# Two attention layers on one core: the steps of layer 1's convolution taps, and of the weight mixes, are set anew

## The chip, the cores and the metric

One core of a Trainium2 chip. The time is that of the whole program on the device, in microseconds. Its engines are TensorE (PE, with its weight loads as PEld), VectorE (DVE), ScalarE (ACT), GpSimd (POOL) and SyncE (SP). Each runs its own queue of instructions in order, and semaphores tie them together. In this kernel SP and POOL issue the DMAs.

## The reference

Two residual layers on an image batch of 4 x 32 x 32 tokens with 768 channels. Each is `x + attention(group_norm(x))` with 12 heads of 64. Layer 0 is plain; layer 1 passes q, k and v through a 3x3 depthwise convolution and a layer norm over each head's 64 channels before it attends. Both add a bias of relative position, by rows and by columns.

```python
# layer 0
q = heads(x @ Wq + bq); k = heads(x @ Wk + bk); v = heads(x @ Wv + bv)
attn = einsum('bqd,bkd->bqk', q, k) / sqrt(HD) + rel_bias_h + rel_bias_w
out = softmax(attn) @ v ; return out @ Wp + bp
# layer 1
q = layer_norm(dwconv3x3(q, w_pool_q), g_q, b_q)    # k and v alike
attn = einsum('bqc,bkc->bqk', q * scale, k) + rel_h + rel_w
o = softmax(attn) @ v + q ; return o @ w_proj.T + b_proj
```

## The kernel before

**Stages and pairs.** There are eight stages, in this order: layer 0 of images 0 and 1, layer 1 of images 0 and 1, then the same for images 2 and 3. A stage has six pairs of heads. Pairs are numbered 0 to 47 over all stages; a pair's index in its stage (`hp`) is that number modulo 6. So layer 1 is pairs 12 to 23 and 36 to 47.

**Steps.** The order on PE, DVE, ACT and POOL is written out by hand. `attend` is a generator that gives a pair's attention in four quarters. A quarter is four score tiles (L1091 with the bias added in L1093), four exponentials (L1098, ACT), and then the product with v (L1115). After the scores it yields twice, and after the product twice, so a pair has 16 steps, and pair i's attention covers the steps 16i to 16i+15. The first quarter of a pair has its steps 0 to 3, and so on. At each step the pieces that `at` has put there are emitted. A piece is work that belongs to a later pair, to the projection of the stage before, to the group norm of the stage after, or to the weights. Pieces of one step are emitted in the order in which they were registered: group norm and token sums first, then the weight mixes, then the pairs' pieces, then the projection's.

**What is prepared when.** `Pair.plan` gives for pair i a list of pieces with steps counted from 16(i-1). So a step of 0 or more lies in the attention of the pair before, and a step of -8 to -1 in the second half of the one before that. In layer 1 that is: q and k by matrix products at -8 to 0, q's nine taps, k's taps, `centre(Q)` at 3 (PE transposes, DVE L721 and L722), `square` and `squares` of q (L728 on ACT, L732 and L733 on DVE), `norm(Q)` at 7 or 8 (the logarithm and exponential L160 and L162 on ACT, then L164 to L167 and L744 on DVE), `back(Q)` at 9 (PE L753, ACT L558 and L559), and the same for k from 8 to 14. `split` (step 12) writes the bias of position in two parts, `high` (L791) and `whole` (L792), which POOL sends to the bias tiles by DMA (L802). v's taps, centring, squares and norm run at 8 to 15.

**The seven products.** Where pair i and the two before it are all of layer 1 (`in_products`; 20 pairs: indexes 2 to 5 of the stage of the first layer-1 image, 0 to 5 of the second, in each half), q and k come from seven products of half-size weights and token sums (`products`, steps -8 or -7 to 0). These need sums of weights ("late" mixes, u = 15 + hp) and sums of tokens in DRAM, read as `blocks` by `call`, L605. With q's padded image complete at -5 (or at -6 for indexes 1 and 4), q's nine taps start: L704 or L702 is the first tap (DVE or ACT), L706 each of the others, over 128 x 1056 elements. A second pair of buffers for the padded image and the convolved one is taken in turn.

**Mixes.** `mix_weights(u)` loads two weight blocks (SP, 384 KB each, into the ring `wproj` of two buffers), and at a later step makes four or five sums or differences of them on DVE (L316 or L328), each of which SP stores to DRAM. u = 0 to 8 are for layer 0's products, 9 to 11 for its projection, 12 to 14 for layer 1's projection, 15 to 20 for layer 1's products. All run once, in the first half of the program: the list at L1295 has for each u the step of the loads and the step of the sums.

**Projection.** In the first 20 steps of a stage the projection of the stage before runs in parts (`four`, `three`; PE L138 with p1p to p7 as output, L1203 and L1198 on DVE, which empty the banks). At the steps 11, 15 and 19 of a stage that leads to or is layer 1, the loop at L1325 puts the pieces marked `taps` of that step between the two parts of the projection.

**Banks.** Score tile 1 of a quarter takes the PSUM area `place_b`, tile 2 `place_c`; between the scores other products use these areas in halves. A score tile therefore waits until the last reader of the halves is done. Tiles 0 and 3 share an area, so tile 3 waits for the first exponential.

**SP's queue** isn't ordered by hand: its order is set by a scheduler when the program is built.

## Time and profile before

| | us |
|---|---|
| time, median of 3 runs (lowest to highest) | 3794.95 (3792.31 to 3801.69) |
| profiled execution, its own time | 3800.9 |
| its span | 3798.9 |

Length of the stages, from the first score matmul of one to that of the next, and how much of it TensorE was idle in gaps over 0.15 us (worked out from the trace's instructions):

| stage (layer, image) | pairs | us | PE idle, us |
|---|---|---|---|
| 1 (0, 1) | 6 to 11 | 464.6 | 5.7 |
| 2 (1, 0) | 12 to 17 | 492.4 | 13.2 |
| 3 (1, 1) | 18 to 23 | 487.3 | 18.4 |
| 5 (0, 3) | 30 to 35 | 460.4 | 3.0 |
| 6 (1, 2) | 36 to 41 | 495.0 | 13.3 |
| 7 (1, 3) | 42 to 47 | 511.8 | 19.7 |

Length of the quarters of some pairs, in us, and the pair's sum:

| pair | index prepared at steps 0 to 15 | quarters | sum |
|---|---|---|---|
| 13 | 2 | 33.8, 13.3, 26.3, 16.1 | 89.5 |
| 14 | 3 | 14.9, 13.3, 26.8, 15.6 | 70.6 |
| 15 | 4 | 18.3, 13.7, 28.7, 15.7 | 76.5 |
| 16 | 5 | 15.6, 13.3, 30.3, 15.6 | 74.8 |
| 17 | 0 | 14.7, 13.3, 26.2, 15.6 | 69.9 |
| 18 | 1 | 19.2, 13.3, 47.5, 38.8 | 118.9 |
| 39 | 4 | 19.8, 13.8, 30.1, 17.3 | 81.0 |
| 45 | 4 | 18.9, 13.3, 27.0, 15.6 | 74.9 |

How to read the profile's lines: in a timeline, the start in us from the span's start, the duration, the engine, the line of the kernel, the operation, what it writes and reads, how many instructions were merged, and in brackets the idle time of the engine before it and what ended it. In a table of windows: the window, its length, then the busy time and (in brackets) the number of instructions of PE, PEld, DVE, ACT and POOL, the granted TensorE clock as a share of full speed, the DMA engines' busy share, and GB/s.

### The profile page before, as it was taken

How to read it: one execution, taken by the hardware profiler on the slowest of the kernel's cores; microseconds unless marked ns; L12 is line 12 of the kernel's file. 1: busy time of each engine (PE TensorE's matmuls, PEld its weight loads, DVE VectorE, ACT ScalarE, POOL GpSimd, SP SyncE). 2: the span in 40 equal slices, each digit the busy share in tenths (PEclk: the TensorE clock that was granted, in tenths of full speed). 3: DMA queues.
4: the chain of work that ended last, by engine and by line, in shares of the span. 5: the costliest groups of instructions: out<-in, count | busy, mean ns of one | idle time of the engine just before them, and what ended most of it. 6: DMA issues, size and time to landing. Idle time of an engine off the chain costs nothing.

```text
span 3798.9 us, 77870 instructions
## 1 busy us (share of the span) xinstructions
PE 3701.1 (97%) x32926; PEld 1644.3 (43%) x32926; DVE 2460.5 (65%) x3179; ACT 1728.7 (46%) x2440; POOL 618.1 (16%) x1152
## 2 busy tenths in 40 slices
PE   8999999999999999999999999999999999999998
PEld 4535535533343443444535445355343444434443
DVE  2566455568678877688444554454686888867884
ACT  2455434545345553355424544254542555534551
POOL 0111000110121231122310010011111122212130
PEclk9999999999999999999999999999999999999999
DMA  4444454442543544442344232523325335354333
GB/s 152 114 130 130 136 160 128 135 140 70 156 140 86 147 131 120 153 113 79 85 121 126 65 86 67 178 66 93 91 66 168 120 101 162 89 151 117 86 91 104
DMA packets 267347, 441.87 MB, mean 116 GB/s; under 512 B 43446, under 2 KB 115538, under 8 KB 266992
## 3 DMA queue, kind: packets, MB, share of 16 engines
q1 hardware_dynamic: 189008, 321.60, 27.2%
q0 software_dynamic: 77984, 115.21, 13.0%
q8 instruction: 263, 4.31, 0.5%
q14 instruction: 92, 0.75, 0.1%
HBM read 275.38 MB, written 60.39 MB: 88 GB/s over the span
## 4 chain that ended last, share of the span: by engine, by line
PE 80%; DVE 11%; issue 3%; DMA 2%; ACT 2%; POOL 1%; SPq 0%; DVEq 0%; ACTq 0%; POOLq 0%
PE av L1115 14%; PE s L1091 14%; PE qkv L138 8%; PE m1m L138 5%; PE m3m L138 4%; PE m4m L138 4%; PE w L138 4%; PE sum L138 4%; DVE shared L706 4%; PE s L1093 3%; PE p3p L138 3%; PE p4p L138 3%; PE rel L775 3%; PE p1p L138 2%; PE m L138 2%
## 5 line engine op out<-in xcount | busy, mean ns | idle before, releaser
L1098 ACT ACTIVATE e<-s 128x1024 f32<-128x1024 f32 x768 | 768.0, 1024 | 368.3 <-PE s L1093 343.7
L1091 PE MATMUL s<-q,k 64*128 64x512 f32 x3072 | 818.4, 609 | 29.9 <-ACT e L1098 16.3
L706 DVE SCALAR_TENSOR_TENSOR shared<-shared,sm 128x1056 f32<-128x1056 f32 x576 | 757.7, 1315 | 14.6
L1093 PE MATMUL s<-bias,ones 64*128 64x512 f32 x1536 | 617.7, 797 | 1.3 <-DMA bias<-high 0.7
L1115 PE MATMUL av<-e,vt 128*64 128x512 f32 x2624 | 600.6, 599 | 0.3
L802 POOL DMA_DIRECT2D bias<-high x384 | 201.8, 541 | 1814.1 <-ACT high L791 1520.3
L1109 DVE TENSOR_TENSOR acc<-acc,e 128x1024 f32<-128x1024 f32 x294 | 360.2, 1225 | 114.1 <-ACT e L1098 88.2
L1091 PEld LDWEIGHTS s<-q,k 64*128 64x128 f32 x3072 | 280.3, 187 | 294.6 <-issue 195.9
L138 PE MATMUL qkv<-xn,wqkv_t 128*64 128x512 f32 x1728 | 386.4, 597 | 0.9 <-DVE xn L408 0.9
L1115 PEld LDWEIGHTS av<-e,vt 128*64 128x64 f32 x2624 | 186.6, 138 | 351.7 <-issue 304.2
L1093 PEld LDWEIGHTS s<-bias,ones 64*128 64x128 f32 x1536 | 150.6, 188 | 187.1 <-issue 179.6
L138 PEld LDWEIGHTS qkv<-xn,wqkv_t 128*64 128x64 f32 x1728 | 120.6, 137 | 235.5 <-issue 229.0
L802 POOL DMA_DIRECT2D bias<-whole x384 | 205.2, 555 | 28.4 <-DVE whole L792 14.2
L593 ACT ACTIVATE shared<-qkv,sm 128x512 f32<-128x512 f32 (+1 forms) x128 | 57.5, 502 | 282.9 <-PE qkv L138 282.9
L938 ACT COPY weighed<-av 128x512 f32<-128x512 f32 x96 | 56.3, 587 | 248.9 <-PE av L1115 248.7
L1107 DVE TENSOR_TENSOR acc<-e 128x1024 f32<-128x1024 f32 x49 | 60.0, 1224 | 150.6 <-PE z L1013 112.2
L721 DVE TENSOR_REDUCE mean<-ln_c 128x8 f32<-128x512 f32 x144 | 98.6, 685 | 76.0 <-PE ln_c L718 76.0
L775 PEld LDWEIGHTS rel<-q,rel 64*32 64x32 f32 x6144 | 112.5, 106 | 69.7 <-issue 54.3
L956 POOL DMA_DIRECT2D inv<-z_inv x94 | 51.7, 554 | 533.4 <-DVE z_inv L950 326.6
L775 PE MATMUL rel<-q_t,rel 64*32 64x32 f32 x6144 | 125.1, 195 | 6.5 <-issue 6.5
L593 ACT ACTIVATE shared<-w,sm 128x512 f32<-128x512 f32 x120 | 53.9, 504 | 165.6 <-DVE w L627 165.6
L775 PE MATMUL rel<-q,rel 64*32 64x32 f32 x6144 | 124.1, 195 | 4.6 <-issue 4.6
(208 smaller groups left out, 5059.1 us busy)
## 6 DMA issues: line engine op xcount, KB each, us to landing
bias<-high POOLq DMA_DIRECT2D x384, 128.0 KB, 3.4
bias<-whole POOLq DMA_DIRECT2D x384, 128.0 KB, 4.3
blocks<-tokens SPq DMA_DIRECT2D x160, 256.0 KB
wqkv_t<-mixed SPq DMA_DIRECT2D x86, 384.0 KB
wqkv_t<-in_wqkv SPq DMA_DIRECT2D x126, 192.0 KB
third_block<-tokens SPq DMA_DIRECT2D x80, 256.0 KB
wproj_t<-mixed SPq DMA_DIRECT2D x48, 384.0 KB
wqkv_t<-in_wqkv SPq DMA_DIRECT2D x38, 384.0 KB
```

The source lines that it names most:

```text
L138: nc.tensor.matmul(ps[lo : lo + D], a[:, lo : lo + D], b, start=start, stop=stop, **kw)
L593: nc.scalar.activation(self.pad[s][:, rows, there : there + src.shape[2]], src, AF.Identity, bias=col(self.column(s)))
L706: nc.vector.scalar_tensor_tensor(y, window, tap, y, ALU.mult, ALU.add)
L721: nc.vector.tensor_reduce(of, heads, AX.X, ALU.add)
L775: nc.tensor.matmul(ps[lo : lo + S, k * S : (k + 1) * S].rearrange("p (b c) -> p b c", b=2), rel[rows, 2 * self.layer + i, first : first + ...
L802: nc.gpsimd.dma_start(sets, some.unsqueeze(1).to_broadcast([D // 2, 2, QC]))
L1091: nc.tensor.matmul(ps[:, j, :], k[rows, keys], q[rows, cols], start=True, stop=False)
L1093: nc.tensor.matmul(ps[:, j, :], ones[rows, kt % 2 * P : (kt % 2 + 1) * P], bias[c][rows, kt // 2, :], start=False, stop=True,)
L1098: nc.scalar.activation(e, ps, AF.Exp)
L1107: nc.vector.tensor_tensor(acc, es[0], es[1], ALU.add)
L1109: nc.vector.tensor_tensor(acc, acc, e, ALU.add)
L1115: nc.tensor.matmul(av[j * D : (j + 1) * D, :], pair.vt[:, kt, j * D : (j + 1) * D], e[:, j, :], start=(kt == 0), stop=(kt == NKT - 1),)
```

## The change

Four things move; no computation is added or dropped.

- q's taps in the 20 pairs with seven products. Before, indexes 1 and 4 had the first tap on ACT at -4, two at -3, one at -2, three at 0 and two at 1, and all others five at -5, two at 0 and two at 1. After, index 2 alone has the first form, and indexes 1 and 4 have five at -5. (`products` itself still treats indexes 1 and 4 in their own way.)
- k's taps 1 to 8 in these pairs start at step 2 in place of 3, two a step.
- The twelve token sums for the first layer-1 stage of each half run at its steps 58 to 66 (counted from the start of the stage before), not at 60 and 64 to 71.
- The mixes u = 17 to 20 come one place earlier, and 15, 14, 16, 12, 13 go from pairs 7 to 11 (layer 0) into pairs 13 to 17 (layer 1).

```diff
             seven = in_products(self.i)
-            early = self.hp in (1, NC // 2 + 1)
+            early = self.hp == 2
             taps = (
                 ((Q, -3, (2, 1, 0, 3, 2)) if early else (Q, -5, (5, 0, 0, 0, 0, 2, 2))) if seven else (Q, -4, (2, 2, 2, 2, 1)),
-                (K, 3 if seven else 2, (2, 2, 2, 2)),
+                (K, 2, (2, 2, 2, 2)),
                 (V, 8, (2, 2, 2, 2)),
             )
...
             token_sums = sum_tokens(stages[k])
-            for r in (60, *range(64, 72)):
+            for r in (60, *range(64, 72)) if stages[k - 1][1] else range(58, 67):
                 at(first + r, lambda token_sums=token_sums: next(token_sums))
...
     for u, call, step in (
         (2, 0, 5), (7, 6, 11), (3, 13, 18), (4, 22, 29), (8, 31, 38), (5, 40, 47), (0, 49, 55), (6, 57, 63), (1, 65, 71),
-        (9, 72, 77), (10, 78, 83), (11, 84, 89), (16, 114, 119), (17, 120, 125), (18, 126, 131), (19, 132, 137),
-        (20, 138, 143), (15, 144, 149), (12, 150, 156), (13, 168, 174), (14, 178, 187),
+        (9, 72, 77), (10, 78, 83), (11, 84, 89), (17, 114, 119), (18, 120, 125), (19, 126, 131), (20, 132, 137),
+        (15, 212, 217), (14, 226, 233), (16, 258, 265), (12, 266, 274), (13, 275, 281),
     ):
```

Instruction by instruction, the order on PE and on POOL is the same in both kernels. On ACT the first tap of q (L702) is added in the four pairs of index 2 and removed in the six of 1 and 4. On DVE the taps, mixes and token sums change places, and on SP the order of many DMAs changes around the moved mixes and token sums.

## The prediction

> **What bounds the kernel now.** The page first, then busy time by window, then the timelines of the windows in which TensorE stops.

> ```profile
> span 3798.9 us, 77870 instructions
> ...
> PE 3701.1 (97%) x32926; PEld 1644.3 (43%) x32926; DVE 2460.5 (65%) x3179; ACT 1728.7 (46%) x2440; POOL 618.1 (16%) x1152
> ...
> PE 80%; DVE 11%; issue 3%; DMA 2%; ACT 2%; POOL 1%; SPq 0%; DVEq 0%; ACTq 0%; POOLq 0%
> ```

> TensorE is idle for 3798.9 - 3701.1 = 98 us, and 80% of the chain that ended last is its own work. The change removes no matmul and leaves TensorE's order as it is, so all that it can win lies in those 98 us and in what follows a stop. DVE is the second link (11%), and nearly every edit moves DVE work.

> The profiled execution took 3798.9 us of span and 3800.9 us in all, 6 us over the 3794.95 us median of the runs shown. I sum differences in that execution and put them on the median.

> Busy time by pair of heads (window, PE, PEld, DVE, ACT, POOL, granted clock, DMA share, GB/s): pairs 10 and 11, then 34 and 35, which do the same work for the second two images without the weight mixes.

> ```profile
> 760.80:837.70 76.90, 74.93 (x614) 28.64 (x612) 45.27 (x56) 34.07 (x49) 11.85 (x20) 1.00 0.51 149
> 837.70:915.50 77.80, 74.83 (x620) 30.54 (x618) 69.57 (x79) 41.16 (x62) 8.32 (x16) 0.98 0.32 92
> ...
> 2642.80:2717.60 74.80, 74.80 (x616) 28.85 (x614) 42.79 (x48) 34.10 (x49) 11.91 (x20) 1.00 0.44 125
> 2717.60:2792.10 74.50, 73.07 (x618) 30.09 (x616) 64.09 (x70) 41.17 (x62) 8.31 (x16) 1.00 0.21 53
> ```

> Pair 10 is 2.1 us longer than 34 and pair 11 3.3 us longer than 35: 5.4 us. The mixes in them are the difference.

> The timeline near the end of pair 12, DVE and then PE. Step 203 holds the five taps of q for index 2.

> ```profile
> 985.91 5.45 DVE L706 SCALAR_TENSOR_TENSOR shared<-shared,sm 128x1056 f32<-128x1056 f32 x4
> ...
> 992.66 0.74 DVE L1198 SCALAR_TENSOR_TENSOR x<-p1p,sm,x 128x512 f32<-128x512 f32 x1
> ```
> ```profile
> 993.46 1.95 PE L1091 MATMUL s<-q,k 64*128 64x512 f32 x4 [2.12 <-DVE x L1198]
> ...
> 997.52 1.94 PE L138 MATMUL w<-blocks,wqkv_t 128*64 128x512 f32 x8
> ```

> DVE has the taps (L704, then four L706) in front of L1198, which empties the projection's bank p1p; the third score tile needs that bank, and TensorE stops for 2.12 us. Then the clock falls (window 993.60 to 997.00, granted clock in the third figure from the end):

> ```profile
> 993.60:997.00 3.40, 3.40 (x12) 1.62 (x12) 0.53 (x1) 1.02 (x1) 0.00 (x0) 0.51 0.68 230
> ```

> The end of pair 44, while index 4 gets three early taps (DVE, then PE):

> ```profile
> 3548.86 2.67 DVE L706 SCALAR_TENSOR_TENSOR shared<-shared,sm 128x1056 f32<-128x1056 f32 x2
> 3554.22 0.18 DVE L164 TENSOR_TENSOR t_ln<-r_ln 128x16 f32<-128x16 f32 x1 [2.69 <-ACT r_ln L162]
> ...
> 3565.15 1.31 DVE L706 SCALAR_TENSOR_TENSOR shared<-shared,sm 128x1056 f32<-128x1056 f32 x1
> 3566.38 1.21 DVE L732 TENSOR_REDUCE lnv<-shared 128x16 f32<-128x1024 f32 x1
> ```
> ```profile
> 3569.26 1.13 PE L1091 MATMUL s<-q,k 64*128 64x512 f32 x4 [2.12 <-ACT e L1098]
> ```

> Taps stand in front of L732 (the variance of v); ACT has the logarithm of it queued before the next pair's exponentials, the fourth score tile needs the first exponential, and TensorE stops again.

> **The change, part by part.** A tap is 1.32 us on DVE (L706; 0.77 for the first, L704) or 1.18 us on ACT (L702).

> *Index 2 (prepared in pairs 12, 18, 36, 42).* The five taps leave step 203 (and the same place in the other three). Then L1198 of p can start at 985.2, that of p1p when its matmuls end (987.0), and both banks are free by 988.6, before the second score tile. From the first score matmul to the product at L138 it took 997.52 - 988.17 = 9.35 us. Undisturbed: 1.81 to the second tile (it waits for L781 as now), 1.08 to each of the next two, 1.3 for the last, about 5.25. So 4.1 us; pairs 18, 36 and 42 took 7.66, 9.07 and 9.86, so 2.4, 3.8 and 4.6: 14.9 us. The taps come back at -4 (one on ACT, where ACT next waits 3.56 us for DVE), -3 (two, 2.67 us), -2 (one) and as five in place of four at steps 0 and 1. The two at -3 precede L1203 of p3p, which has 0.68 us of idle before it: the product that overwrites its bank slips from 1009.04 to about 1009.45, 0.4 us four times. The one at -2 falls into 7.02 us of DVE idle, the fifth at 0 and 1 into 2.39. Net -13.3. Bounds: -6.9 (the bare 2.12 us four times, less 1.6) to -18 (four times the best).

> [...]

> *Indexes 1 and 4 (ends of pairs 14, 20, 38, 44 and of 17 and 41).* Three DVE taps leave the place ahead of L732, and one on ACT; five go to -5. There q's padded image is complete at 3548.55 (L593), but L732, L733 and two taps of v hold DVE to 3551.53. The five take 0.77 + 4 x 1.32 + gaps = 6.2 us, to 3557.8. The normalization of k (L164 on) waited for ACT until 3554.22, so only 2.7 us of the five are hidden and it starts 3.6 us later. Behind it are L792 (the bias that goes out by DMA), L627 and L593 (the bank of w5, which TensorE's next product reuses), and the centring of v, now ending at 3565.1 instead of 3561.3. The squares on ACT then end near 3566.4, L732 runs at 3566.6 to 3567.8 and the first exponential starts at about 3568.5, where it was 3568.20. What the three taps gave, the five take: the stop changes its waiter (L593 or the bias in place of e) and stays. +0.25 each, +1.5 for six. Bounds: a gain of 24 if the stop goes (the first quarter of pairs 15, 21, 39, 45, 18 and 42 fell from 18.3, 18.3, 19.8, 18.9, 19.2 and 18.9 us to the 14.7 to 15.2 of their neighbours); a loss of 2 each, 12, if the late bias adds to it.

> *k's taps from step 2 (20 pairs).* Two taps (2.67 us) move ahead of the centring of q (L721), which most often has DVE idle before it: 2.69 in pair 15, 3.57 in 17, 7.75 in 13, and the bank read by L722 has 1.2 us to spare before the third score tile. Where they don't fit, that tile is late: pair 14 (group statistics and a wait for z_inv fill the idle) 1.9, 18 1.1, 42 0.7, 40 0.95, 16 0.45: +5.1. Two taps fewer stand between L733 and the normalization of q, for which L753 made TensorE wait 1.45 to 1.5 us in pairs 15, 16, 18, 21, 39, 40 and 1.06 in 42, and in front of L718 in pair 14 (0.54): -10.5. All eight taps now precede L732, whose logarithm ACT does before the exponentials: 1.2 us later in 16 and 40, where DVE is never free, 0.3 in 18 and 42: +3.0. Net -2.4. Bounds -10 to +5.

> *Mixes.* u = 15, 14, 16, 12, 13 go from pairs 7 to 11 into 13 to 17 (17 to 20 move up by one place within 7 and 8). Off layer 0: 5.4 us above and 0.4 of pair 9, -5.8. In layer 1 each is four or five subtractions or sums of 0.55 us, 2.2 to 2.8 us on DVE. Idle near their new steps: 3.03 in pairs 13 and 16, 2.6 in 14, 3.57 and 2.93 in 17; only step 274 shares its idle with k's two taps (1.7 over, 0.5 after the slack). Their DMAs: two loads of 384 KB and four or five stores of 192 KB on SP, ahead of or between the block loads. Those are just in time (blocks issued at 1086.69 to 1088.78, last needed at 1093.76), and SP puts the mix's first load and wqkv_t ahead of the second block: 384 KB at the 263 GB/s of a busy window (1496 to 1502), 1.5 us, of which I take 0.7 for five places: +3.5 with the above +4. Net -1.8; bounds -6 to +9.

> *Token sums at 58 to 66 (pairs 9, 10, 33, 34).* Same twelve sums of 0.69 us; the stretch of 8.1 us at the end of pair 9 gets five beside 4.9 us of L1109. Before, five such sums in a 9.4 us stretch made no stop. +1; bounds 0 to +5.

> Sum: -13.3 + 1.5 - 2.4 - 1.8 + 1 = -15.0 us; 3794.95 - 15.0 = 3780 us.

> **Rivals.**
> *Indexes 1 and 4 are freed.* If five taps at -5 are hidden there as they are for indexes 3 and 5 (pairs 14, 16, 38 and 40, which follow such ends, begin with quarters of 14.7 to 15.6 us), 24 us more: 3780 - 1.5 - 24 = 3754. Against: for 3 and 5 the padded image was there 0.85 us before the scores began (1246.63 against 1247.48), here 0.6 us after.
> *Slower.* The 3.6 us delay of L792 and L593 adds to the stop rather than replacing it, in all six places, and the clock falls behind each (1.7 us): 5.3 x 6 = 32, 3780 - 1.5 + 32 = 3810 us. For it: the first bias's last transfer landed between 0.5 us before and 1.2 us after the first score matmul of those six pairs, so it has no slack. Against: the exponentials waited until 4.6 us after that matmul anyway. It decides from 2.8 us a place ((15.0 + 1.5) / 6).
> *The stop of index 2 only moves*: the two taps at -3 hold the projection's L1203 and L1198 for their whole 2.67 us and the clock falls there: nothing won, 3793. For: L1203 has 0.68 us. Against: the idle right behind, 1.82 and then 7.02 us.
> *The mixes don't fit layer 1*: block loads late by two loads, 3 us at five places in place of the 4 above: 3780 - 4 + 15 = 3791.

> **How the numbers follow.** A measurement of this kernel tells 0.3% (11.4 us) from no change: 3783.6 to 3806.3. Forecast 0.62, freed 0.12, slower 0.10, moved 0.09, mixes 0.07. The forecast's own range is 3768 to 3791; I give 0.68 of it to below 3783.6. Faster 0.42 + 0.12 + 0.02 + 0.02 = 0.58; slower 0.08 of its rival and 0.04 of the others, 0.12; same 0.30. The range runs to 3760 (most of the gain of the freed places) and to 3800 (the stop moved, with the mixes near their dear end).

> **What would show it.** Right: no PE stop on L1198 of p1p at the ends of pairs 12, 18, 36 and 42, clock 1.0 there, and that stretch near 5.3 us; a stop of about 2 us still in the first scores of pairs 15, 18, 21, 39, 42 and 45, now behind L593, the bias or k; no wait of L753 on L744 in pairs 15, 21, 39; pairs 10 and 11 as long as 34 and 35. Wrong: quarters of 15 us in those six pairs (then freed), or over 20 us (then slower).

## The result, and the profile after

| | before | after |
|---|---|---|
| time, median of 11 runs (lowest to highest), us | 3796.08 (3792.31 to 3801.69) | 3783.68 (3778.08 to 3789.89) |
| span of the profiled execution, us | 3798.9 | 3781.5 |
| PE idle in gaps over 0.15 us, in that execution, us | 76.6 | 71.2 |
| time at half clock in it, without a stretch at the very end, us | 37.5 | 13.7 |

The ratio is 0.9967, with a 95% interval of 0.9958 to 0.9976: 12.4 us less, where the prediction had 15.0 less. Within 2% the two kernels count as the same; against the 0.3% that the prediction named as the bound, the ratio lies just on the faster side, and its interval reaches over the bound.

The page of the changed kernel, the same lines of it that the prediction shows of the kernel before:

```profile
span 3781.5 us, 77865 instructions
...
PE 3688.4 (98%) x32926; PEld 1640.7 (43%) x32926; DVE 2463.0 (65%) x3181; ACT 1724.8 (46%) x2438; POOL 617.4 (16%) x1152
...
PE 82%; DVE 10%; issue 3%; DMA 3%; ACT 1%; POOL 1%; SPq 0%; DVEq 0%; ACTq 0%; POOLq 0%
```

PE has the same 32926 matmuls, but is busy 12.7 us less. A matmul at half clock counts as busy for longer (the four score matmuls behind the stop at 993.46 took 1.95 us; four such take 1.13 us below), so this is clock time, not work. It fits the table above: 37.5 - 13.7 = 23.8 us fewer at half clock, half of it lost, 11.9 us; and 5.4 us less idle. Together 17.3 us, which is the whole difference of the two spans (17.4).

The end of pair 12 in the changed kernel, a timeline of PE and then a window of busy times:

```profile
984.04 1.13 PE L1091 MATMUL s<-q,k 64*128 64x512 f32 x4
...
985.80 1.13 PE L1091 MATMUL s<-q,k 64*128 64x512 f32 x4 [0.41 <-ACT whole L781]
...
989.27 1.94 PE L138 MATMUL w<-blocks,wqkv_t 128*64 128x512 f32 x8
```
```profile
990.50:997.30 6.80, 6.80 (x36) 2.63 (x34) 6.30 (x12) 3.20 (x7) 4.38 (x9) 1.00 0.84 244
```

The stop on L1198 is gone. From the first score matmul to the product at L138 it takes 989.27 - 984.04 = 5.23 us (9.35 before; the prediction had 5.25), and the granted clock behind it is 1.00, where it was 0.51.

The stages, by the same measure as before: 459.9 us for stage 1 (464.6 before), 495.7 for 2 (492.4), 483.0 for 3 (487.3), 460.7 for 5 (460.4), 487.7 for 6 (495.0) and 507.1 for 7 (511.8). The quarters that changed most:

| place | before, us | after, us | change |
|---|---|---|---|
| last quarters of pairs 12, 18, 36, 42 (index 2) | 38.5, 38.8, 38.4, 39.7 | 34.7, 36.4, 34.7, 34.7 | -14.9 |
| end of 14, 20, 38, 44 and start of the next (index 4) | 33.9, 33.9, 35.4, 34.5 | 35.8, 33.5, 33.6, 32.5 | -2.3 |
| end of 17 and 41 and start of the next (index 1) | 34.8, 34.5 | 39.4, 39.1 | +9.2 |
| third quarters of 14, 15, 16, 18, 21, 39, 40, 42 (k's taps) | 268.1 in all | 260.0 in all | -8.1 |
| second quarters of 14, 16, 40 (k's taps) | 39.9 in all | 43.0 in all | +3.1 |

Stage 2 got longer although pair 12 lost 3.8 us: the ends of pairs 14 and 17 took 4.5 and 2.2 us more (the first with a half-clock stretch), with 2.6 less at the start of pair 15, and two second quarters took 2.1 more.

### The profile page after: what moved, and what is told of

Same layout as the page of the kernel before. It is cut to its first block, busy times and chain, and to the rows that moved or that the text cites. A ratio compares the mean times of both kernels' runs of the same rounds, so it can differ in the third digit from the quotient of the medians.

```text
span 3781.5 us, 77865 instructions
## 1 busy us (share of the span) xinstructions
PE 3688.4 (98%) x32926; PEld 1640.7 (43%) x32926; DVE 2463.0 (65%) x3181; ACT 1724.8 (46%) x2438; POOL 617.4 (16%) x1152
## 4 chain that ended last, share of the span: by engine, by line
PE 82%; DVE 10%; issue 3%; DMA 3%; ACT 1%; POOL 1%; SPq 0%; DVEq 0%; ACTq 0%; POOLq 0%
PE s L1091 15%; PE av L1115 14%; PE qkv L138 9%; PE m1m L138 5%; PE m3m L138 4%; PE m4m L138 4%; PE sum L138 4%; PE s L1093 4%; PE w L138 4%; PE p3p L138 3%; PE p1p L138 3%; PE rel L775 3%; DVE shared L706 2%; PE p4p L138 2%; PE m L138 2%
## 5 line engine op out<-in xcount | busy, mean ns | idle before, releaser
L1098 ACT ACTIVATE e<-s 128x1024 f32<-128x1024 f32 x768 | 767.3, 1023 | 357.7 <-PE s L1093 332.8
L1091 PE MATMUL s<-q,k 64*128 64x512 f32 x3072 | 811.2, 604 | 13.1 <-ACT e L1098 4.7
L706 DVE SCALAR_TENSOR_TENSOR shared<-shared,sm 128x1056 f32<-128x1056 f32 x576 | 757.5, 1315 | 14.9
L1109 DVE TENSOR_TENSOR acc<-acc,e 128x1024 f32<-128x1024 f32 x294 | 360.2, 1225 | 117.1 <-ACT e L1098 90.9
L1091 PEld LDWEIGHTS s<-q,k 64*128 64x128 f32 x3072 | 279.7, 186 | 276.2 <-issue 195.0
L138 PE MATMUL qkv<-xn,wqkv_t 128*64 128x512 f32 x1728 | 387.3, 598 | 0.9 <-DVE xn L408 0.9
L138 PEld LDWEIGHTS qkv<-xn,wqkv_t 128*64 128x64 f32 x1728 | 121.1, 138 | 236.5 <-issue 230.7
L593 ACT ACTIVATE shared<-qkv,sm 128x512 f32<-128x512 f32 (+1 forms) x128 | 57.4, 502 | 284.2 <-PE qkv L138 284.2
L775 PEld LDWEIGHTS rel<-q,rel 64*32 64x32 f32 x6144 | 112.8, 106 | 74.6 <-issue 60.0
L593 ACT ACTIVATE shared<-w,sm 128x512 f32<-128x512 f32 x120 | 53.8, 503 | 196.4 <-DVE w L627 196.4
L775 PE MATMUL rel<-q,rel 64*32 64x32 f32 x6144 | 124.3, 195 | 8.5 <-issue 8.5
L721 DVE TENSOR_REDUCE mean<-ln_c 128x8 f32<-128x512 f32 x144 | 98.6, 685 | 48.3 <-PE ln_c L718 48.3
L775 PE MATMUL rel<-q_t,rel 64*32 64x32 f32 x6144 | 125.2, 195 | 4.4 <-issue 4.4
```

The lines of the kernel that those rows point to most:

```text
L138: nc.tensor.matmul(ps[lo : lo + D], a[:, lo : lo + D], b, start=start, stop=stop, **kw)
L593: nc.scalar.activation(self.pad[s][:, rows, there : there + src.shape[2]], src, AF.Identity, bias=col(self.column(s)))
L706: nc.vector.scalar_tensor_tensor(y, window, tap, y, ALU.mult, ALU.add)
L721: nc.vector.tensor_reduce(of, heads, AX.X, ALU.add)
L775: nc.tensor.matmul(ps[lo : lo + S, k * S : (k + 1) * S].rearrange("p (b c) -> p b c", b=2), rel[rows, 2 * self.layer + i, first : first + ...
L1091: nc.tensor.matmul(ps[:, j, :], k[rows, keys], q[rows, cols], start=True, stop=False)
```

## The experiments

Ten kernels: one for each of five parts of the change on top of the kernel before, then five forms of the changed kernel. Quarters and stops are those of the one profiled execution of each kernel; a ratio is that of the timed runs to those of the kernel before, with its 95% interval.

### Index 2 alone

```diff
-            early = self.hp in (1, NC // 2 + 1)
+            early = self.hp in (1, 2, NC // 2 + 1)
```

> The kernel before with one change: index 2's q taps in the form first tap on ACT at -4, two at -3, one at -2, three at 0, two at 1. Theory (the stop on L1198 at the ends of pairs 12, 18, 36, 42 goes and does not come back): the last quarters of these four pairs fall from 38.5, 38.8, 38.4 and 39.7 us to 34.7, 36.4, 34.7 and 34.7 as in the changed kernel, -14.9 us together, the taps at -3 add up to 0.4 us each, so about -13 in all, ratio near 0.9965. Rival (the stop only moves, and the rest of the change made the gain): the quarters before or behind lengthen by as much, total within 3 us of before.

Measured: ratio 0.9966 (0.9955 to 0.9976), 12.9 us less (9.1 to 17.1). The four quarters went to 34.7, 36.4, 34.7 and 34.7: 14.9 us less, as in the changed kernel. The stop didn't move elsewhere, so the rival falls. One part of the change by itself gives all that the whole gave.

### Indexes 1 and 4 alone

```diff
-            early = self.hp in (1, NC // 2 + 1)
+            early = False
```

> The kernel before with one change: indexes 1 and 4 get five taps of q at -5, as all others have; index 2 stays as it was. Theory: at index 4 (pairs 14/15, 20/21, 38/39, 44/45) the stop moves from the first exponential to the small bank that L593 empties, the end of the pair before grows from 15.6 to 17.8 us and the first quarter falls from 18.3 to 19.8 us to about 15.7, -0.6 us each on average; at index 1 (17/18, 41/42) the end grows to 17.8 and the first quarter to about 21.5, +4.6 us each. Sum about +7 us, ratio near 1.002. The prediction's own term was +1.5 (+0.25 in each of six). Rival (freed): first quarters near 15 us and no longer ends, -24 us.

Measured: ratio 1.0005 (0.9996 to 1.0014), +1.9 us (-1.5 to +5.3). The +7 of the expectation, formed after the result, lies outside that interval; the prediction's +1.5 lies inside. At index 4 the stop moved as expected: end and start together 33.6, 33.6, 33.6 and 34.2 us, -2.7 in all (1.8 of it at pair 39, whose start had a half-clock stretch before). At index 1 the ends grew to 19.5, but the starts fell to 15.6 and 16.4: +0.3 and +1.4, not +4.6 each. So five taps at -5 don't by themselves cost what index 1 costs in the changed kernel. The product at L989 in pair 18 shows it; PE in this kernel, then in the changed one:

```profile
1422.48 0.66 PE L989 MATMUL last<-weighed,cst 128*64 128x256 f32 x4 [0.59 <-ACT shared L593]
```
```profile
1420.27 1.12 PE L989 MATMUL last<-weighed,cst 128*64 128x256 f32 x4 [5.05 <-ACT shared L593]
```

### k's taps alone

```diff
-                (K, 3 if seven else 2, (2, 2, 2, 2)),
+                (K, 2, (2, 2, 2, 2)),
```

> The kernel before with one change: k's taps from step 2 in place of 3 in the 20 pairs. Theory: the third quarters of pairs 15, 16, 18, 21, 39, 40 and 42 fall by 1 to 1.7 us each (no wait of L753 on L744), about -10 us, and the second quarters of pairs 14, 16, 18, 40 and 42 grow by 0.5 to 1.9 us (the third score tile behind L722), with later exponentials in some: net -2.4 us, ratio near 0.9994. Rival: the later L722 costs as much as L753 gave or more, 0 to +5 us.

Measured: ratio 0.9995 (0.9986 to 1.0004), -1.9 us (-5.3 to +1.5), which doesn't tell it from nothing. The quarters went both ways, as expected, most of them by more: third quarters of 15, 16, 18, 21, 39, 40 and 42 by -0.7, -2.1, -1.6, -2.5, -2.6, -1.9 and -1.2, but the second of 18, 42, 14 and 16 by +2.5, +1.8, +1.4 and +1.0; that of 40 stayed. Together that is -5.9 us in this execution, more than the timed runs show. In pair 18's second quarter the third score tile waits for L722 (PE):

```profile
1427.78 1.09 PE L1091 MATMUL s<-q,k 64*128 64x512 f32 x3 [2.29 <-DVE shared L722]
```

### The mixes alone

The diff is that of the list of mixes, as shown with the change.

> The kernel before with one change: the list of weight mixes (17 to 20 one place earlier, 15, 14, 16, 12 and 13 in pairs 13 to 17). Theory: pairs 9, 10 and 11 lose 0.8 + 0.6 + 3.1 us as in the changed kernel, about -4.5, and pairs 13 to 17 gain 0.7 to 1 us each where blocks come later behind the mix's loads, +3: net -1.8 us, ratio near 0.9995. Rival (the mixes do not fit layer 1): pairs 13 to 17 gain 3 us each, net +9. Second rival (they cost nothing in layer 1): -4.5 or more.

Measured: ratio 0.9998 (0.9989 to 1.0007), -0.8 us (-4.2 to +2.7). Of layer 0 the quarters of pairs 9, 10 and 11 fell by 0.5, 2.2 and 3.2, 5.9 in all; pairs 12 to 17 of layer 1 grew by 3.2. What was won in layer 0 was half given back. The rival of 3 us in each of five pairs falls: the largest growth, in pair 16, is 1.6.

### The token sums alone

```diff
-            for r in (60, *range(64, 72)):
+            for r in (60, *range(64, 72)) if stages[k - 1][1] else range(58, 67):
```

> The kernel before with one change: the twelve token sums ahead of the first layer-1 stage of each half at steps 58 to 66. Theory: pair 34's first quarter grows by 1.5 us and pair 10's by about 1.3 (a stop of some 1.2 us behind the token sum L475), pair 33 falls by 0.5: +1 to +2.5 us, ratio near 1.0004. Rival (the earlier sums let the first blocks of layer 1 land earlier and the layer-1 pairs 12 and 36 gain by it): below 0, pairs 12 and 36 shorter by over 0.5 us.

Measured: ratio 1.0015 (1.0006 to 1.0024), +5.7 us (2.3 to 9.1), dearer than expected. Pair 34's first quarter grew by 1.7, as expected; the surprise is pair 10's, which went from 28.9 to 34.2. DVE and PE there:

```profile
767.25 0.69 DVE L352 TENSOR_TENSOR token_sum<-xn 128x512 f32<-128x512 f32 x1
...
770.09 0.69 DVE L352 TENSOR_TENSOR token_sum<-xn,token_sum 128x512 f32<-128x512 f32 x1 [1.43 <-DMA tokens<-token_sum]
...
773.50 2.55 DVE L1109 TENSOR_TENSOR acc<-acc,e 128x1024 f32<-128x1024 f32 x2
...
777.30 0.68 DVE L475 TENSOR_TENSOR shared<-shared,m3m 128x512 f32<-128x512 f32 x1
```
```profile
778.03 4.54 PE L138 MATMUL m3m<-xn,wqkv_t 128*64 128x512 f32 x10 [4.61 <-DVE shared L475]
```

A token sum waits 1.43 us for the store of an earlier one, the sums and then L1109 stand in front of L475, and L475 frees PE's bank 4.61 us late. The kernel before has a stop of 1.97 us at this place already, so 2.6 of the 5.3 us are the longer stop; the other 2.7 are clock, a stretch of 6.83 us at half speed that begins at 776.50 and reaches 5.3 us past the stop. A mix (L328) ends just before, at 767.3; in the changed kernel that mix is elsewhere, and the stop at this place is 1.29 us, though the sums wait longer for earlier stores (PE, then DVE):

```profile
774.85 1.51 PE L138 MATMUL m3m<-xn,wqkv_t 128*64 128x512 f32 x6 [1.29 <-DVE shared L475]
```
```profile
764.97 0.69 DVE L352 TENSOR_TENSOR token_sum<-token_sum,xn 128x512 f32<-128x512 f32 x1 [3.74 <-DMA tokens<-token_sum]
765.84 0.69 DVE L352 TENSOR_TENSOR token_sum<-xn,token_sum 128x512 f32<-128x512 f32 x1 [0.17 <-DMA tokens<-token_sum]
767.78 0.69 DVE L352 TENSOR_TENSOR token_sum<-xn 128x512 f32<-128x512 f32 x1 [1.25 <-DMA tokens<-token_sum]
```

The parts alone add up to -12.9 + 1.9 - 1.9 - 0.8 + 5.7 = -8.0 us; the whole gave -12.4. The intervals of the five measurements, 3 to 4 us to each side for each, could hide that difference. In the profiled executions this place makes most of it: its quarter costs 5.3 us with the sums alone and, against the 26.7 us of the mixes alone, 1.5 with both.

### Index 1 put back

```diff
-            early = self.hp == 2
+            early = self.hp in (1, 2)
```

> The changed kernel with one change: index 1's q taps get the earlier form too (as in the kernel before), index 2 keeps it, index 4 keeps five at -5. Theory: the ends of pairs 17 and 41 fall from 17.8 to 15.6 us and the first quarters of 18 and 42 from 21.6 and 21.3 to 19.2 and 18.9, so -4.6 us in each place, -9 us against the changed kernel, about 3775 us, ratio to the kernel before near 0.994. Rival (the stop's size is no matter of the taps, index 1 is dear for another cause, for instance the mixes in pair 17 or k's earlier taps): less than 3 us won, ratio near 0.9965.

Measured: ratio 0.9961 (0.9947 to 0.9976), some 2 us under the changed kernel's 0.9967, within the intervals; the 9 us were not there, and the figure is the rival's. The ends and starts fell (17.8 and 21.6 to 16.3 and 17.5; 17.8 and 21.3 to 15.6 and 18.8), but the second quarters of 18 and 42 rose from 13.3 to 15.9 and 17.0, behind L722. PE in pair 18:

```profile
1425.22 1.09 PE L1091 MATMUL s<-q,k 64*128 64x512 f32 x3 [2.30 <-DVE shared L722]
```

These are the stops that k's taps made alone. In the earlier form five taps of q follow L950 where the changed kernel has four, and k's two stand behind them, ahead of L721. So index 1's two forms cost nearly the same here, each in its own place.

### The last part of the products earlier for index 1

```diff
-                steps = (-8 if early_late else -7, -6, -4, -2, 0)
+                steps = (-8 if early_late else -7, -6, -4, -2, -1 if self.hp == 1 else 0)
```

> The changed kernel with one change: for index 1 the last part of the seven products (which ends in L627 and the L593 of the small bank) runs at step -1 in place of 0, so ahead of L950, the reciprocal in the stage's first pair, which waits for a DMA queued on POOL behind the bias. Theory (index 1 was dear because L627 stands on DVE behind L950): the stops of 5.05 and 4.66 us at the product L989 in pairs 18 and 42 go or fall below 2.5 us, and these pairs' starts are shorter by 2 to 4 us each, -4 to -8 us against the changed kernel, ratio to the kernel before near 0.995. Rival (L627 is late by the five taps alone, whatever stands in front of it): the stop keeps its size or moves to the end of pairs 17 and 41, within 2 us of the changed kernel.

Measured: ratio 0.9959 (0.9945 to 0.9973), 3 us under the changed kernel by the ratios, less than expected and again inside the intervals. The stops of 5.05 and 4.66 us at L989 are gone, and the first quarters of 18 and 42 fell by 3.3 and 4.6. In their place the exponentials come late, 3.32 and 1.66 us in the first scores; PE in pair 18:

```profile
1409.76 1.13 PE L1091 MATMUL s<-q,k 64*128 64x512 f32 x4 [3.32 <-ACT e L1098]
...
1414.53 0.60 PE L989 MATMUL last<-weighed,cst 128*64 128x256 f32 x4
```

So L627 behind L950 was what held L989 there, and ahead of it another wait shows.

### Index 1 put back, and the token sums as before

The changed kernel with index 1 put back as above, and with the line of the token sums as in the kernel before.

> The changed kernel with two changes: index 1's q taps in the earlier form as well, and the token sums ahead of layer 1 at 60 and 64 to 71 as in the kernel before. Theory: -9 us for index 1, and a further -1 to -3 for the token sums (pairs 10 and 34 lose their 1.2 us stops), about 3773 us, ratio to the kernel before near 0.9935. Rival: the token sums are worth nothing, then the same time as with index 1 alone.

Measured: ratio 0.9953 (0.9939 to 0.9967), 5 us under the changed kernel by the ratios. The 0.9935 expected is outside, since the 9 us for index 1 in it didn't come. The token sums' part did, at its upper end: the stops in pairs 10 and 34 are gone (first quarters 26.7 and 26.7, from 28.2 and 28.2), 3.0 us.

### A third form for index 4, and for index 1

The first of two kernels takes the one above and gives index 4 two taps at -5 and five at step 0. The second has index 1 in a form of its own as well, two at -5 and three at -1, with the earlier last part of the products.

```diff
-                ((Q, -3, (2, 1, 0, 3, 2)) if early else (Q, -5, (5, 0, 0, 0, 0, 2, 2))) if seven else (Q, -4, (2, 2, 2, 2, 1)),
+                ((Q, -3, (2, 1, 0, 3, 2)) if early else (Q, -5, (2, 0, 0, 0, 0, 5, 2) if self.hp == 4 else (5, 0, 0, 0, 0, 2, 2))) if seven else (Q, -4, (2, 2, 2, 2, 1)),
```

> The changed kernel with index 1's q taps in the earlier form and the token sums as before, and for index 4 a third form of q's taps: two at -5, five at 0, two at 1 (in place of five, two, two). Theory (five taps at -5 hold the normalization of k, and with it L792, L627, L593 and the squares of v, back by some 3.5 us, because only two of them are hidden): with two the small bank is free in time and the exponentials are not late either, so the ends of pairs 14, 20, 38 and 44 fall from 17.8 to 20.1 us to 15.6 and the first quarters of 15, 21, 39 and 45 from 15.7 to 14.7, -3 us in each place, -12 us against the changed kernel for index 4 and about -6 for the rest: about 3766 us, ratio to the kernel before near 0.992. Rival (the three taps at step 0 are late there: the stop moves to the second quarter, behind L722, or to L950 and L593): those pairs' first two quarters grow by 2 us or more each, ratio near 0.995.

Measured: ratio 0.9932 (0.9919 to 0.9945), median 3771.63 us, 8 us under the kernel above by the ratios, with intervals that just overlap. The ends of pairs 14, 20, 38 and 44 are 16.1, 15.6, 15.6 and 15.6 us: the stop is gone. The first quarters that follow stayed at 15.7, 15.8, 15.7 and 14.7, where 14.7 was expected of all. The second quarters grew by 0.6 to 1.1 (behind L722, 0.4 to 0.9 us), a small part of what the rival said. The end of pair 44, DVE and PE, first in the changed kernel:

```profile
3537.23 5.45 DVE L706 SCALAR_TENSOR_TENSOR shared<-shared,sm 128x1056 f32<-128x1056 f32 x4
3542.60 0.17 DVE L164 TENSOR_TENSOR t_ln<-r_ln 128x16 f32<-128x16 f32 x1
...
3546.31 0.69 DVE L627 TENSOR_TENSOR w<-w,temps 128x512 f32<-128x512 f32 x1
```
```profile
3548.04 1.94 PE L138 MATMUL w<-blocks,wqkv_t 128*64 128x512 f32 x8 [2.10 <-ACT shared L593]
```

and in this one:

```profile
3522.49 1.32 DVE L706 SCALAR_TENSOR_TENSOR shared<-shared,sm 128x1056 f32<-128x1056 f32 x1
3524.47 0.17 DVE L164 TENSOR_TENSOR t_ln<-r_ln 128x16 f32<-128x16 f32 x1 [0.66 <-ACT r_ln L162]
...
3528.19 0.69 DVE L627 TENSOR_TENSOR w<-w,temps 128x512 f32<-128x512 f32 x1
```
```profile
3531.13 1.94 PE L138 MATMUL w<-blocks,wqkv_t 128*64 128x512 f32 x8
```

With five taps L164 starts the moment DVE is free; with two it waits 0.66 us for ACT, and all that follows it is in time.

The second kernel's edits to the first:

```diff
-                steps = (-8 if early_late else -7, -6, -4, -2, 0)
+                steps = (-8 if early_late else -7, -6, -4, -2, -1 if self.hp == 1 else 0)
...
-            early = self.hp in (1, 2)
+            early = self.hp == 2
...
-                ((Q, -3, (2, 1, 0, 3, 2)) if early else (Q, -5, (2, 0, 0, 0, 0, 5, 2) if self.hp == 4 else (5, 0, 0, 0, 0, 2, 2))) if seven else (Q, -4, (2, 2, 2, 2, 1)),
+                ((Q, -3, (2, 1, 0, 3, 2)) if early else (Q, -5, (2, 0, 0, 0, 0, 5, 2) if self.hp == 4 else (2, 0, 0, 0, 3, 2, 2) if self.hp == 1 else (5, 0, 0, 0, 0, 2, 2))) if seven else (Q, -4, (2, 2, 2, 2, 1)),
```

> As the other kernel of this call, and index 1 in a third form as well: two taps at -5, three at -1, two at 0, two at 1, with the last part of the seven products at -1, ahead of the reciprocal L950. Theory: of what index 1 costs, the late L593 of the small bank and the late exponentials go (ends of 17 and 41 at 15.6 us), and the wait for L950, 8 to 11 us behind the first score matmul, no longer holds L627: first quarters of 18 and 42 from 18.6 and 18.0 us to 15 to 16, second quarters from 14.3 and 15.9 to 13.3 to 14; -6 to -9 us against the other kernel, ratio to the kernel before near 0.990. Rival (the product at L989 or the taps behind L950 need the reciprocal itself): first quarters stay near 18 us, the ratio of the other kernel.

Measured: ratio 0.9921 (0.9908 to 0.9935), median 3767.39 us, the fastest of all, 29 us under the kernel before in its own comparison. The gain over the other kernel is some 4 us, inside the intervals, and smaller than expected: first quarters of 17.5 and 17.5, not 15 to 16, and second quarters of 14.2 and 15.0, not 13.3 to 14. ACT and then PE at the start of pair 18:

```profile
1398.75 0.22 ACT L162 ACTIVATE r_ln<-ln_ln 128x16 f32<-128x16 f32 x1
1401.91 0.89 ACT L593 ACTIVATE shared<-w,sm 128x512 f32<-128x512 f32 x2 [2.94 <-DVE w L627]
1402.66 3.77 ACT L1098 ACTIVATE e<-s 128x1024 f32<-128x1024 f32 x4
```
```profile
1403.74 0.70 PE L1091 MATMUL s<-q,k 64*128 64x512 f32 x2 [2.53 <-ACT e L1098]
```

Moved to -1, L593 stands on ACT ahead of the exponentials, and waits there for L627. The piece that was freed of one wait became another's.

## Why the prediction came out as it did

**What bounds the kernel** held: PE's work is unchanged, and the difference lies in its stops and in the clock behind them. Profiled, 5.4 us of 17.4 are stops and 11.9 are clock. The medians moved by less, 12.4 us: the execution that was profiled before took 3800.9 us, 4.8 over the median of its kernel, and the one after was at its median.

**Index 2** (-14.9 gross, -13.3 net) is right in mechanism, place and size: the four last quarters have the same lengths in every kernel with this edit, 14.9 us less than before, and the timed runs of the edit alone give 12.9 less (9.1 to 17.1). The stretch up to the product at L138 is 5.23 us in all four pairs, 15.0 less together. The slip behind L1203 is 0.26 us in three pairs and nothing in pair 18, 0.8 in all where 1.6 was put down; another 0.9 us of clock lay behind the stretch in pairs 36 and 42. The clock behind the stops went with them: three of the four were followed by 3.4, 3.4 and 6.8 us at half speed (pairs 12, 36 and 42), half of it lost, some 6.8 us, and the changed kernel has no such stretch at these ends.

**Indexes 1 and 4** (+1.5): alone, +1.9 (-1.5 to +5.3). That the stop stays and changes its waiter, from e to L593, is what the trace shows (its place is the end of the pair before, not the first scores that the prediction named), and that the five taps hold L164 is confirmed by the kernel with two, which loses the stop. But inside the whole change it is -2.3 for index 4 (two half-clock stretches before, one after, are in this) and +9.2 for index 1, and the step "+0.25 each" was wrong for index 1, because it treated the six places alike. Pairs 18 and 42 are the first of their stage, where L950 waits for a DMA and stands on DVE ahead of the L627 that L989 needs by way of L593. The DVE timeline of the changed kernel:

```profile
1411.35 0.07 DVE L746 MEMSET vt<- 128x16 f32 x1
1418.10 0.34 DVE L950 RECIPROCAL z_inv<-z_inv 32x32 f32<-32x32 f32 x1 [6.67 <-DMA z_inv<-z]
...
1418.61 0.68 DVE L627 TENSOR_TENSOR w<-w,temps 128x512 f32<-128x512 f32 x1
```

The DMA's chain (z, then z_inv) is issued by POOL behind the sixteen transfers of the bias. Before, the same chain let L989 run 12.4 and 12.2 us behind the pair's first score matmul, and the stop on the exponential, 2.12 and 1.94 us, lay inside that time (PE of the kernel before, pair 18):

```profile
1413.49 2.08 PE L1091 MATMUL s<-q,k 64*128 64x512 f32 x4 [2.12 <-ACT e L1098]
...
1420.28 0.66 PE L989 MATMUL last<-weighed,cst 128*64 128x256 f32 x4 [0.24 <-ACT shared L593]
```

Of two waits that ran side by side one was taken out of the pair and put in the pair before, where it costs 2.2 us (in pair 17 most of it shows as a stop of 1.40 us behind L706), and the other stayed, now in full view: 5.05 and 4.66 us, with L989 at 13.3 and 12.9 us. L989 is only 0.8 and 0.6 us later than before; the rest of the 2.4 us by which each first quarter grew is clock. Before, the half-clock stretch lay ahead of L989, where the wait hid it; now it lies behind. With the taps alone the chain was done early (L989 at 8.8 and 9.6 us behind the first score matmul) and this wait didn't show. The traces give two differences: the end of the pair before had a half-clock stretch more, which puts the first score matmul 1.7 us later against DVE and POOL, and z took 4.8 us to land in place of 7.4. What made that transfer slower in the whole change was not tried; it stays open. Nor are the 9.2 us what this part costs in the whole: with index 1 put back the timed runs are some 2 us faster, since k's taps make stops in its place.

**k's taps** (-2.4): -1.9 (-5.3 to +1.5). The sum lies inside the interval, though both of its halves were too small: L722's stops in pairs 18 and 42 came to 2.3 and 1.6 us where 1.1 and 0.7 were put down, and the third quarters gave more too.

**Mixes** (-1.8): -0.8 (-4.2 to +2.7). Layer 0 gave 5.9 for the 5.8 predicted, and layer 1 took 3.2 of the 4.

**Token sums** (+1, bounds 0 to +5): alone +5.7, over the upper bound, but with a mix at the same place that the whole change takes away. In the whole change pairs 10 and 34 show stops of 1.29 and 1.21 us and first quarters 1.5 us longer each than with the sums put back: +3.0, inside the bounds. The stretch at the end of pair 9 was measured by its length, 8.1 us, and the sums by their 0.69 us; left out was that a sum waits for an earlier sum's store (3.74, 0.17 and 1.25 us in pair 10 of the changed kernel), so that five of them take longer than their own time.

**The sum.** That it came out 2.6 us from the forecast is partly luck. In the profiled execution index 1 cost 8.7 us more than its two shares of the term, while index 4, k's taps and index 2 gave 3.3, 2.6 and 1.6 us more than theirs.

**The rivals.** "Freed" didn't come about, but part of the gain it spoke of was there to be had at index 4 with two taps in place of five: ends and starts of 124.8 us together, from 137.7 before, less 3.2 in the second quarters. The rival named the right stop and the wrong edit. At index 1 no form that was tried won anything: in the fastest kernel ends and starts are 2.1 us shorter than before, and second quarters 2.6 longer. "Slower" fell; what comes nearest to it is index 1, where the delay did add a wait. "Moved" and "don't fit" fell by the runs with index 2 and the mixes alone.

**What would have shown it.** Three of the four signs named as right came: no stop on L1198, no wait of L753 on L744 in pairs 15, 21 and 39 (stops of 2.20, 1.40 and 1.41 us remain there, ahead of L775, 0.43, 1.30 and 1.85 before, which the profile puts down to no other engine), pairs 10 and 11 at 76.3 and 74.6 us against the 74.8 and 74.5 of 34 and 35 before, with 1.5 us of the former due to the token sums. The fourth, a stop of about 2 us behind L593, came at index 4 but ahead of the first scores, so the first quarters of 15, 21, 39 and 45 fell to 15.7, 15.7, 15.8 and 14.7: by itself the sign for "freed", and only the longer ends of the pairs before tell the two apart. The sign for "slower", first quarters over 20 us, came in 18 and 42.

## What to carry to other kernels

Before a stop is moved, ask which second wait it covers: one that ends at the same time or a little earlier costs nothing until the first is gone (L989 in pair 18: 0.24 us before, 5.05 after). Where work must pass an engine in order, split it at the point where the hidden part ends (two taps of five here), and put the rest behind the instructions that others wait for. Measure the parts of a bundled change one by one: here one part in five gave the whole gain, one alone cost nearly half as much as that, and two forms of a third cost much the same, each in another place.

## What the runs showed of the clock

| PE idle within one window | windows | followed by one at half clock |
|---|---|---|
| 0.5 to 1.7 us | 496 | 3 |
| 1.7 to 2.0 us | 35 | 16 |
| 2.0 us and more | 54 | 54 |

The kernels before and after have, in these three rows, 91 windows with 1 followed by half clock, 7 with 5, and 9 with 9 (idle time in gaps over 0.15 us).

The windows of two stops, busy times with the clock in the third figure from the end. In the changed kernel a stop of 2.17 us lies inside one window; in the kernel with the earlier last part of the products, a stop of 3.32 us lies across two:

```profile
1177.80:1181.20 3.40, 1.23 (x8) 0.48 (x8) 3.37 (x6) 1.79 (x4) 2.80 (x6) 1.00 0.50 95
1181.20:1184.60 3.40, 3.40 (x10) 0.73 (x6) 3.29 (x6) 1.84 (x3) 3.40 (x8) 0.50 0.96 235
```
```profile
1404.60:1408.00 3.40, 1.84 (x12) 0.71 (x8) 2.61 (x7) 0.43 (x3) 0.40 (x1) 1.00 1.08 333
1408.00:1411.40 3.40, 1.64 (x8) 0.69 (x10) 0.00 (x0) 3.40 (x6) 0.54 (x1) 1.00 0.53 156
1411.40:1414.80 3.40, 3.40 (x20) 1.20 (x18) 2.18 (x4) 2.12 (x3) 1.08 (x2) 1.00 0.07 11
```

The first leaves PE busy for 1.23 of 3.40 us, and the next window has a clock of 0.50; the second leaves 1.84 and 1.64, and the clock stays at 1.00. Of the eight stops named above, the three with a halved clock behind them had 1.97 us or more inside one window, the other five 1.78 us or less. So they cost their own length, or some 1.7 us more (half of 3.4 us) where all or nearly all of a stop lay in one window. It fits a part of the spread between runs of one kernel: of the eleven of the changed kernel, the two longest (3789.2 and 3789.9 us) had a mean clock of 0.996, the two shortest (3778.1 and 3779.1) 0.997 and 0.998, though one of 3782.0 us had 0.996 too.
